# Loading and stepping the first block's odd spectra during the last chunk of a Fourier filter kernel

## The chip, the cores and the metric

The kernel runs on one core of a Trainium2 chip, in float32, as one launch. The metric is the device time of the whole kernel in microseconds (us): the median of three runs.

## What is computed

The input is an image batch of 4 x 56 x 56 positions with 128 channels. Layer 0 is a neighbourhood attention block (7 x 7 windows, four heads) with a dense block behind it. Layer 1 reads the same values as 3136 tokens for each of 4 images. It adds a small attention term and then a spectral filter, and it is the last part of the filter that matters here:

```python
Vf = jnp.fft.rfft(phi, n=n, axis=0)
Uf_p = jnp.fft.rfft(u, n=n, axis=1)
Uf_m = jnp.fft.rfft(u * sgn3, n=n, axis=1)
U_plus = jnp.fft.irfft(Vf[None, :, :, None] * Uf_p[:, :, None, :], n=n, axis=1)[:, :sl]
U_minus = jnp.fft.irfft(Vf[None, :, :, None] * Uf_m[:, :, None, :], n=n, axis=1)[:, :sl]
...
out = jnp.einsum('btkd,k,kde->bte', U_plus, s, Mpp)
out = out + jnp.einsum('btkd,k,kde->bte', U_minus, s, Mpm)
```

So the tokens are transformed to frequencies, at each frequency multiplied by 16 filters and mixed over the channels by matrices, and transformed back. Four such filters with different lengths are weighed and added to the tokens.

## The kernel before, in words

All engines have their own queues and wait for each other by semaphores: PE (matmuls), DVE, ACT and POOL (elementwise work), SP (DMA issue only). ACT issues DMAs too, in line with its other work. Every DMA that SP or ACT issues takes the next of eight semaphores in turn, and its issue waits until the DMA that had this semaphore before has landed. Hence at most eight are on their way.

**Chunks.** The 245 frequencies are worked off in 31 chunks of eight (`NCH = 31`, `FC = 8`). For chunk c, `fetch_tokens` (L1045) loads the transformed tokens into a tile `xc` (four loads of 256 KB on ACT, two tiles in turn), `tokens` (L1062, POOL) takes them apart into `v`, `make` (L1094) builds the frequency's matrices `g`: PE multiplies the filters `ph` with the mixing matrices `mc` into PSUM banks `pg`, and DVE and ACT copy them out. `product` (L1127) multiplies `v` and `g` into banks `py`. DVE forms sums and differences `ys`, and they are stored to the spectra `yd` in device memory (L1158): index 0 of `yd` for even spectra, 1 for odd ones. The loop at L1225 interleaves, in eight steps u, `make` of chunk c + 1 with `product` of chunk c. `g` lies in two large places in turn.

**The way back.** The rest is the inverse transform, for two blocks ("pair" 0 and 1) of two filters ("j") each. It needs all frequencies, in two halves of 128 ("fh" 0 and 1, from frequency 0 and from 117, so only half 1 needs the last chunk). For each block the odd spectra come first, then the even ones (L1350). `fetch_back` (L1172) brings one block, parity and half: eight loads of 512 KB on SP into a ring tile, which takes the place of a `g`: ring 0 (half 0) that of chunk 29, ring 1 (half 1) that of chunk 30. `odd` and `even` (L1273, L1257) do butterfly steps on DVE, in place: four operations of 128 x 1024 for each j of an odd half, and eight of 128 x 2048 down to 128 x 512 for each j of an even one. `products` (L1283) multiplies them on PE with tables of waves into eight PSUM banks: for the odd part 8 phases x 4 matmuls for each half, for the even part 8 x 2. Half 0 goes through all phases first, half 1 then closes the banks, and DVE adds each closed bank to the tokens in a tile `xo` (L1305). That sum frees the bank for the next part. The tables come through ACT: the odd table of half 0 takes the place of the mixing matrices `mc` (L1186), that of half 1 the tile `io`, the two even ones the tiles `ie`. `xo` is loaded by SP and stored by ACT (L1309).

**What sets the order.** Up to the first steps of the chunks the order is that of the code. After `order.close()` (L1223) a scheduler places the instructions on each queue by its own reckoning, except those marked with `keep_in_program_order` (the token loads, L1054). In the last chunk (c = 30) the loop's else-branch asks for the odd table of half 0 and for ring 0: odd, then even (L1232 to L1235):

```python
waves_back[0] = odd_waves(0, 0)
ring_tile()
for par in (1, 0):
    ready[par] = fetch_back(0, par, 0)
```

Of the kernel before, what the change touches and what calls it, by code (L numbers as in the profile page):

```python
# [9 lines left out]
FP = mybir.dt.float32  # L10
AF = mybir.ActivationFunctionType
ALU = mybir.AluOpType
AX = mybir.AxisListType
PSUM = bass.MemoryType.PSUM
DRAM = bass.MemoryType.DRAM

B, H, W, C = 4, 56, 56, 128
# [27 lines left out]
L = N // PH  # L45
R = NF // PH
RT = (0, R - C)
# [3 lines left out]
NCH = -(-R // FC)  # L51
SKIP = NCH * FC - R
FB = 4
CW = FC * PH * 2
# [6 lines left out]
def conv_attn_hybrid_kernel(ctx: ExitStack, tc: tile.TileContext, a: dict, out: bass.AP):  # L61
    nc = tc.nc
# [7 lines left out]
    yd = dram.tile([2, R, C + 8, C], FP, name="yd")  # L70
# [972 lines left out]
    filters_in, fetched, made, spectra, sums = {}, {}, {}, {}, {}  # L1043

    def fetch_tokens(c, j=None):  # L1045

        n = NP * B
        if c not in fetched:
            fetched[c] = cp.tile([C, n, CW], FP, tag="xc", name=f"xc{c}")
        x = fetched[c]  # L1050
        src = ud.rearrange("j b c w -> c (j b) w")[:, :, CW * c : CW * (c + 1)]
        if j is not None:
            part = slice(B * j, B * (j + 1))
            load = nc.scalar.dma_start(x[:, part], src[:, part])  # L1054
            if c > 1:
                tc.keep_in_program_order(load)
            return

        for part in (slice(n - B), slice(n - B, n)):
            nc.sync.dma_start(x[:, part], src[:, part])  # L1060
# [103 lines left out]
    ring, ready, waves_back = [], {}, {}  # L1164
# [4 lines left out]
        pool = gpools[(NCH + len(ring)) % 2]  # L1169
        ring.append(pool.tile([C, 2, 4, 2, PAIR], FP, tag="g", name=name))  # L1170

    def fetch_back(pair, par, fh):  # L1172
        y = ring[fh][:, 1 - par]

        for m in range(4):
            for r in range(2):
                row = 16 * (2 * m + r) + 8 * pair
                nc.sync.dma_start(
                    y[:, m, r],
                    yd[par, RT[fh] : RT[fh] + C, row : row + 8].rearrange("f n e -> f (n e)"),  # L1180
                )
        return y.rearrange("f m s (j x) -> f j m s x", j=2)

    def odd_waves(pair, fh, pool=None):
        if pool is None:
            t = mc.rearrange("c e d -> c (e d)")[:, : 32 * L]  # L1186
        else:
            t = pool.tile([C, 32 * L], FP, tag="io", name=f"io_{pair}_{fh}")
        nc.scalar.dma_start(t, a["itab_odd"][pair, fh])
        return t.rearrange("f (j k m r p n) -> f j k m r p n", j=2, k=2, m=2, r=2, p=2)  # L1190

    chunks = ExitStack()
    with tc.tile_pool(name="last", bufs=1, side="right") as own, tc.tile_pool(
        name="weigh", bufs=1, side="right"
# [9 lines left out]
        run(extra)  # L1204


    cp = chunks.enter_context(tc.tile_pool(name="w3", bufs=2, side="right"))
    filters_of(0)
    fetch_tokens(0)
# [4 lines left out]
    front.close()  # L1214

    gpools = [ctx.enter_context(tc.tile_pool(name=f"wg{i}", bufs=1)) for i in range(2)]
    ps_g = chunks.enter_context(tc.tile_pool(name="ps_g", bufs=6, space=PSUM))
    ps_y = chunks.enter_context(tc.tile_pool(name="ps_y", bufs=2, space=PSUM))
    for u in range(8):
        make(0, u)  # L1220
        if u % 2:
# [2 lines left out]
    PIECES = (1, 2, 5, 6)  # L1224
    for c in range(NCH):  # L1225
        if c + 1 < NCH:
            if (c + 1) % FB == 0:
                filters_of((c + 1) // FB)
            tokens(c + 1)
        else:  # L1230

            waves_back[0] = odd_waves(0, 0)  # L1232
            ring_tile()
            for par in (1, 0):
                ready[par] = fetch_back(0, par, 0)  # L1235
        for u in range(8):
            if c + 1 < NCH:
                make(c + 1, u)

                if c + 2 < NCH and u in PIECES:  # L1240
                    fetch_tokens(c + 2, PIECES.index(u))
            product(c, u)
    chunks.close()


    tokens_out = out.rearrange("b n p c -> b (n p) c")
    with tc.tile_pool(name="w4", bufs=1) as wp, tc.tile_pool(
        name="ps_t", bufs=8, space=PSUM
    ) as ps_t:
        ring_tile()  # L1250

        def butterfly(u, v):

            nc.vector.tensor_tensor(u, u, v, ALU.add)
            nc.vector.scalar_tensor_tensor(v, v, -2.0, u, ALU.mult, ALU.add)

        def even(y):  # L1257

            butterfly(
                y[:, :2].rearrange("f m s x -> f (m s) x"),  # L1260
                y[:, 2:].rearrange("f m s x -> f (m s) x"),
            )
            butterfly(y[:, 0], y[:, 1])
            butterfly(y[:, 2, 0], y[:, 3, 1])
            butterfly(y[:, 2, 1], y[:, 3, 0])
            return (
                [y[:, 0, 0], y[:, 0, 1]],
                [y[:, 3, 1], y[:, 2, 1]],
                [y[:, 1, 0], y[:, 1, 1]],
                [y[:, 2, 0], y[:, 3, 0]],  # L1270
            )

        def odd(y):  # L1273


            butterfly(y[:, :2, 0], y[:, 2:, 1])
            butterfly(y[:, :2, 1], y[:, 2:, 0])
            return (
                [y[:, 2, 1], y[:, 0, 1], y[:, 3, 1], y[:, 1, 1]],
                [y[:, 0, 0], y[:, 2, 0], y[:, 1, 0], y[:, 3, 0]],  # L1280
            )

        def products(pair, phases, terms, xos, dst):  # L1283


            banks = {}
            for fh in range(2):
                for j, p, *what in phases:
                    if fh == 0:
                        banks[j, p] = ps_t.tile([L, B, C], FP, tag="t", name=f"pi_{pair}_{j}_{p}")  # L1290
                    of = terms(fh, j, *what)
                    for k, (it, z) in enumerate(of):
                        nc.tensor.matmul(  # L1293
                            banks[j, p],
                            it,
                            z,
                            start=(fh == 0 and k == 0),
                            stop=(fh == 1 and k == len(of) - 1),
                        )
                    yield  # L1300
                    if fh == 0:
                        continue
                    xo = xos[j][:, :, p, :]
                    o = 2 * pair + j
                    nc.vector.scalar_tensor_tensor(  # L1305
                        xo, banks[j, p], on[:L, o : o + 1], xo, ALU.mult, ALU.add
                    )
                    if dst and p == 6:
                        nc.scalar.dma_start(dst[j], xos[j].rearrange("n b p e -> n b (p e)"))  # L1309
# [6 lines left out]
        for pair in range(2):  # L1316
# [7 lines left out]
            ys, xos = {}, []  # L1324
            ios = [
                waves_back[0] if pair == 0 else odd_waves(pair, 0),
                odd_waves(pair, 1, wp),
            ]
# [3 lines left out]

            def even_loads():
                for fh in range(2):
                    t = wp.tile([C, 16 * L], FP, tag=f"ie{fh}", name=f"ie_{pair}_{fh}")
                    nc.scalar.dma_start(t, a["itab_even"][pair, fh])
                    ies.append(t.rearrange("f (j p r n) -> f j p r n", j=2, p=4, r=2))
                ys[0, 0] = fetch_back(pair, 0, 0) if pair else ready[0]
                ys[0, 1] = fetch_back(pair, 0, 1)
                for j in range(2):  # L1340
                    xo = wp.tile([L, B, PH, C], FP, tag=f"xo{j}", name=f"xo_{pair}_{j}")
                    for b in range(B):
                        nc.sync.dma_start(
                            xo[:, b].rearrange("n p e -> n (p e)"), here[j][:, b]
                        )
                    xos.append(xo)
# [3 lines left out]
            for par, step, phases in ((1, odd, odd_phases), (0, even, even_phases)):  # L1350
                zs = {}
                for fh in range(2):
                    for j in range(2):
                        zs[fh, j] = step(ys[par, fh][:, j])
                        for _ in range(4):
                            next(behind, None)
                for _ in behind:
                    pass
                if par and pair:
                    even_loads()  # L1360

                def terms(fh, j, *what, zs=zs, ios=ios, ies=ies):
                    if len(what) > 1:
                        kind, i = what
                        return [
                            (ios[fh][:, j, kind, m, r, i], zs[fh, j][kind][2 * m + r])
                            for m in range(2)
                            for r in range(2)
                        ]
                    return [(ies[fh][:, j, what[0], r], zs[fh, j][what[0]][r]) for r in range(2)]  # L1370

                behind = products(pair, phases, terms, xos, None if par else into)
# [108 lines left out]
```

## Time and profile before

| | us |
|---|---|
| three runs: median (lowest to highest) | 1965.07 (1964.43 to 1971.44) |
| the profiled execution: its own time / its span | 1977.2 / 1975.4 |
| mean granted TensorE clock over the span | 0.976 of full speed |
| busy: PE / weight loads / DVE / ACT / POOL | 1885.4 / 1225.9 / 1202.1 / 1023.8 / 908.6 |
| steady chunks, for each 25 us from 1700 to 1775: PE / DVE busy | 24.8 to 25.0 / 17.9 to 18.4 |
| way back, 1775 to 1975: mean rate of the loads while they run | 240 to 409 GB/s |

Durations, waits and DMA shares come from one profiled execution; the median comes from runs without the profiler. A group in a view reads: start, duration, engine, line, operation, tiles written and read, shape, count, and in brackets the idle time ahead of it with what ended it. PE work on float32 stands in the profile as two records for each matmul of the code. PEld is PE's weight load, DVEq and the like the engine's queue.

### The profile page before, as it was taken

The page shows a single profiled execution, that of the slowest core. Times are in us where ns is not written, and L with a number is a line of the kernel's source. Part 1 is how long each engine was busy: PE and PEld are TensorE (multiplying, and loading weights), DVE is VectorE, ACT ScalarE, POOL GpSimd, SP SyncE. Part 2 cuts the span into 40 slices and gives each one's busy share as a digit, 9 for nine tenths or more (in the row PEclk, how much of TensorE's full clock was granted, in tenths as well). Part 3 has the DMA queues.
Part 4 walks back from the last instruction along what each step waited for, and adds up shares of the span by engine and source line. Part 5 has one row for each costly group of instructions (what it writes and reads, how often), then busy time and mean ns, then how long its engine had stood idle before and what let it go on. Part 6 is the DMA issues. An engine that isn't in the chain of part 4 may idle for free.

```text
span 1975.4 us, 57869 instructions
## 1 busy us (share of the span) xinstructions
PE 1885.4 (95%) x24220; PEld 1225.9 (62%) x24220; DVE 1202.1 (61%) x2749; ACT 1023.8 (52%) x2311; POOL 908.6 (46%) x1441
## 2 busy tenths in 40 slices
PE   7998999999999999999999999899999999996998
PEld 4555555565555565555565445788888888883333
DVE  3765644455645456544565664677777777765983
ACT  2666675556685656675555433455555555550000
POOL 2443321365321565222473026788888887770000
PEclk9898999899999999999999999999999999998999
DMA  3122000054000153000254628344444444449981
GB/s 104 33 89 68 2 1 1 19 182 158 2 1 1 31 198 129 1 1 1 83 172 158 203 80 294 99 126 132 126 130 127 126 131 125 128 140 392 355 308 66
DMA packets 184848, 223.48 MB, mean 113 GB/s; under 512 B 13016, under 2 KB 161561, under 8 KB 181996
## 3 DMA queue, kind: packets, MB, share of 16 engines
q1 hardware_dynamic: 107792, 129.07, 20.9%
q10 hardware_dynamic: 74444, 57.70, 9.4%
q0 software_dynamic: 2352, 33.01, 4.2%
q8 instruction: 191, 3.13, 0.6%
q14 instruction: 69, 0.57, 0.1%
HBM read 141.77 MB, written 77.97 MB: 111 GB/s over the span
## 4 chain that ended last, share of the span: by engine, by line
PE 78%; issue 7%; DVE 6%; DMA 5%; ACT 3%; POOL 1%; SPq 0%; ACTq 0%; DVEq 0%; POOLq 0%
PE pg L1103 14%; PE py L1139 13%; PE pi L1293 6%; PE px L716 5%; PE ppt L825 4%; PE pl L769 4%; PE ph L557 3%; PE pf L548 3%; PE par L650 3%; PE pav L882 3%; PE pv L845 3%; DMA ring<-yd 1%; DMA ud<-ab 1%; PE pav L430 1%; PE pk L489 1%
## 5 line engine op out<-in xcount | busy, mean ns | idle before, releaser
L809 POOL TENSOR_SCALAR p<-p,den 112x280 f32<-112x280 f32 x448 | 214.8, 497 | 481.0 <-PE ppt L825 226.6
L1121 DVE COPY g<-pg 128x512 f32<-128x512 f32 (+1 forms) x496 | 319.7, 690 | 147.3 <-PE pg L1103 147.2
L1119 ACT COPY g<-pg 128x512 f32<-128x512 f32 (+1 forms) x496 | 263.9, 584 | 232.9 <-PE pg L1103 232.9
L1103 PE MATMUL pg<-ph,mc 32*128 32x128 f32 x7936 | 296.2, 284 | 5.7 <-DVE g L1121 5.7
L796 ACT ACTIVATE p<-p,low 112x280 f32<-112x280 f32 x448 | 231.1, 517 | 94.0 <-DVE low L782 93.6
L1103 PEld LDWEIGHTS pg<-ph,mc 32*128 32x128 f32 x7936 | 248.4, 187 | 46.1 <-issue 37.3
L1139 PE MATMUL py<-g,v 128*32 128x128 f32 x7840 | 274.6, 281 | 1.3 <-issue 1.0
L1139 PEld LDWEIGHTS py<-g,v 128*32 128x32 f32 x7840 | 219.2, 152 | 30.5 <-issue 1.8
L782 DVE CUSTOM_DVE_ANT_0 p<-pl,bias 112x280 f32<-112x280 f32 x448 | 174.8, 445 | 15.1 <-PE pl L769 3.1
L832 DVE COPY pt<-ppt 120x448 f32<-120x448 f32 x112 | 69.3, 619 | 111.3 <-PE ppt L825 110.5
L825 PEld LDWEIGHTS ppt<-ident,p 112*120 112x120 f32 x896 | 99.6, 138 | 59.9 <-issue 39.6
L825 PE MATMUL ppt<-ident,p 112*120 112x112 f32 x896 | 127.5, 263 | 8.5 <-POOL p L809 4.1
L724 POOL TENSOR_TENSOR ab<-ab,w 128x496 f32<-128x496 f32 x60 | 74.6, 1243 | 105.4 <-ACT w L723 60.6
L716 PE MATMUL px<-tab,tok 98*128 98x496 f32 x256 | 117.8, 606 | 5.4 <-ACT tok L710 3.2
L832 ACT COPY pt<-ppt 120x448 f32<-120x448 f32 x224 | 87.1, 444 | 48.8 <-PE ppt L825 48.7
L769 PE MATMUL pl<-kt,qt 32*112 32x280 f32 x896 | 96.0, 444 | 11.9 <-ACT qt L508 5.7
L557 PE MATMUL ph<-ln_m,w_fc 128*128 128x448 f32 x224 | 102.5, 548 | 1.6 <-DVE ln_m L538 1.5
L548 PE MATMUL pf<-h,w_fc 128*128 128x448 f32 x224 | 100.8, 540 | 0.0
L565 ACT ACTIVATE h<-ph,b_fc 128x448 f32<-128x448 f32 x112 | 69.3, 633 | 60.5 <-PE ph L557 58.7
L882 PE MATMUL pav<-pt,v 120*32 120x112 f32 x1792 | 87.4, 267 | 0.0
L570 DVE SCALAR_TENSOR_TENSOR x<-pf,b_fc,x 128x448 f32<-128x448 f32 x28 | 19.1, 684 | 112.0 <-PE pf L548 112.0
L716 PEld LDWEIGHTS px<-tab,tok 98*128 98x128 f32 x256 | 48.6, 198 | 56.6 <-issue 42.2
(241 smaller groups left out, 3403.3 us busy)
## 6 DMA issues: line engine op xcount, KB each, us to landing
ring<-yd SPq DMA_DIRECT2D x64, 512.0 KB
ud<-ab POOLq DMA_DIRECT2D x16, 1984.0 KB, 8.8
xc<-ud ACTq DMA_DIRECT2D x120, 256.0 KB
tab<-in_tab SPq DMA_DIRECT2D x160, 189.9 KB
yd<-ys SPq DMA_DIRECT2D x118, 256.0 KB
mat<-in_M_phi_plus SPq DMA_DIRECT2D x16, 512.0 KB
mat<-in_M_phi_minus SPq DMA_DIRECT2D x16, 512.0 KB
x<-in_x SPq DMA_DIRECT2D x28, 224.0 KB
```

The source lines that it names most:

```text
L548: nc.tensor.matmul(po[:, :GT], late["w_fc2"][:, i, :], hts[g - 1][i], start=(i == 0), stop=(i == 3),)
L557: nc.tensor.matmul(ph[:, :GT], w_fc1[:, i * C : (i + 1) * C], lnm[:, g * GT : (g + 1) * GT], start=True, stop=True,)
L716: nc.tensor.matmul(ps, toks[i // 4][:, i % 4, :], next(tab), start=True, stop=True)
L769: nc.tensor.matmul(pls[h][:TQ, :KEYS], qts[b, g][hs, t * TQ : (t + 1) * TQ], kt[hs, r0 : r0 + KR, c0 : c0 + KC], start=True, stop=True,)
L782: nc.vector.tensor_tensor_reduce(out=f["p"][:, h, :], in0=f["pls"][h][:TQ, :KEYS], in1=bias[:, h, :], scale=-1.0, scalar=3.0e38, op0=ALU.a ...
L796: nc.scalar.activation(f["p"][:, h, :], f["p"][:, h, :], AF.Exp, bias=f["low"][:, h : h + 1], scale=-1.0, accum_out=f["den"][:, h : h + 1],)
L809: nc.gpsimd.tensor_scalar(f["p"][:, h, :], f["p"][:, h, :], f["den"][:, h : h + 1], 1.0, ALU.mult, ALU.mult)
L825: nc.tensor.transpose(ppt[:, i, :], of, ident[:TQ, :TQ])
L1103: nc.tensor.matmul(banks[rg][:, q, :], mc[r, 4 * u + q, :], t[r, at : at + CW], start=True, stop=True,)
L1119: nc.scalar.copy(into, src)
L1121: nc.vector.tensor_copy(into, src)
L1139: nc.tensor.matmul(py[32 * m : 32 * m + 32, f - f0, :], weights(v, 1 - r, f, slot), g[:, (2 * slot + r) * FC + f, :], start=(r == 0), stop ...
```

## The change

The odd spectra of block 0, half 0, j = 0 (eight pieces of 256 KB) are no longer part of ring 0. They go to two tiles `early0` and `early1` of the pool that holds the tokens `xc`, which now outlives the chunks. The four pieces of `early0` are loaded by ACT during chunk 29's products, at the four steps where the token loads of a further chunk would stand; the four of `early1` by SP at the start of the last chunk. Their steps are two butterflies, one ahead of the last chunk's loop and one after its step u = 5, both kept in program order on DVE, as are the steps of j = 1. Ring 0 keeps the pieces of j = 1. The even spectra of half 0 are asked for behind the odd ones of half 1 in the code. The odd table of half 0 is loaded in two pieces, the even tables take the places of the token tiles (so of `early0` and `early1`), and the inverse matmuls use the banks of the chunks' two PSUM pools instead of a pool of their own.

In the issue order of the changed program, everything up to the last chunks stands as before. On SP, `early1`'s four loads stand ahead of the stores of chunk 29's first sums; then come the eight smaller loads of ring 0, four even loads of ring 0, eight odd loads of ring 1, the other four even ones of ring 0, and the rest as before. On DVE the steps of `early0` stand ahead of the last chunk's first sums and those of `early1` ahead of its last sums.

```diff
-            fetched[c] = cp.tile([C, n, CW], FP, tag="xc", name=f"xc{c}")
+            fetched[c] = xp.tile([C, n, CW], FP, tag="xc", name=f"xc{c}")
...
+    def spectrum_of(par, fh, m, r, at, n):
+        row = 16 * (2 * m + r) + at
+        of = yd[par, RT[fh] : RT[fh] + C, row : row + n]
+        return of.rearrange("f n e -> f (n e)")
...
-    def fetch_back(pair, par, fh):
+    def fetch_back(pair, par, fh, first=0):
         y = ring[fh][:, 1 - par]
         for m in range(4):
             for r in range(2):
-                row = 16 * (2 * m + r) + 8 * pair
                 nc.sync.dma_start(
-                    y[:, m, r],
-                    yd[par, RT[fh] : RT[fh] + C, row : row + 8].rearrange("f n e -> f (n e)"),
+                    y[:, m, r, first * C :],
+                    spectrum_of(par, fh, m, r, 2 * B * pair + first, 2 * B - first),
                 )
...
+    halves = {}
+    def fetch_early(half, queue, i):
+        if half not in halves:
+            halves[half] = xp.tile([C, 4, B * C], FP, tag="xc", name=f"early{half}")
+        r = half if i < 2 else 1 - half
+        load = queue.dma_start(halves[half][:, i], spectrum_of(1, 0, i, r, 0, B))
+        if half == 0:
+            tc.keep_in_program_order(load)
...
+        n = 32 * L // parts
+        for part in range(parts):
+            here = slice(n * part, n * (part + 1))
+            nc.scalar.dma_start(t[:, here], a["itab_odd"][pair, fh][:, here])
...
+    def butterfly(u, v, hold=lambda i: i):
+        hold(nc.vector.tensor_tensor(u, u, v, ALU.add))
+        hold(nc.vector.scalar_tensor_tensor(v, v, -2.0, u, ALU.mult, ALU.add))
...
+    xp = ctx.enter_context(tc.tile_pool(name="xc", bufs=2, side="right"))
...
-            waves_back[0] = odd_waves(0, 0)
+            for i in range(4):
+                fetch_early(1, nc.sync, i)
+            waves_back[0] = odd_waves(0, 0, parts=2)
             ring_tile()
-            for par in (1, 0):
-                ready[par] = fetch_back(0, par, 0)
+            ready[1] = fetch_back(0, 1, 0, first=B)
+            butterfly(halves[0][:, :2], halves[0][:, 2:], tc.keep_in_program_order)
...
+                elif c + 2 == NCH and u in PIECES:
+                    fetch_early(0, nc.scalar, PIECES.index(u))
             product(c, u)
+            if c + 1 == NCH and u == 5:
+                butterfly(halves[1][:, :2], halves[1][:, 2:], tc.keep_in_program_order)
+    z0, z1 = ([h[:, i] for i in range(4)] for h in (halves[0], halves[1]))
+    first = [z0[2], z1[0], z0[3], z1[1]], [z0[0], z1[2], z0[1], z1[3]]
...
-                        banks[j, p] = ps_t.tile([L, B, C], FP, tag="t", name=f"pi_{pair}_{j}_{p}")
+                        pool, tag = (ps_g, "g") if len(banks) < 6 else (ps_y, "y")
+                        banks[j, p] = pool.tile([L, B, C], FP, tag=tag, name=f"pi_{pair}_{j}_{p}")
...
-                    t = wp.tile([C, 16 * L], FP, tag=f"ie{fh}", name=f"ie_{pair}_{fh}")
+                    t = xp.tile([C, 16 * L], FP, tag="xc", name=f"ie_{pair}_{fh}")
...
-                ys[0, 0] = fetch_back(pair, 0, 0) if pair else ready[0]
+                ys[0, 0] = fetch_back(pair, 0, 0)
...
-                        zs[fh, j] = step(ys[par, fh][:, j])
+                        if (pair, par, fh, j) == (0, 1, 0, 0):
+                            zs[fh, j] = first
+                            continue
+                        behind_sums = (pair, par, fh) == (0, 1, 0)
+                        hold = {"hold": tc.keep_in_program_order} if behind_sums else {}
+                        zs[fh, j] = step(ys[par, fh][:, j], **hold)
```

## The prediction

> **What bounds the kernel now.** I read first the table of busy time by stretch, to see which engine fills the tail, then the timeline of the tail, then the chain of work that ended last. Up to 1773 us the two programs issue the same work, but for eight small loads, so only the last 200 us matter.
>
> ```profile
> 1750.00:1775.00 25.00, 24.78 (x734) 21.53 (x732) 17.86 (x28) 13.56 (x25) 17.94 (x23) 1.00 0.45 139
> 1775.00:1800.00 25.00, 9.39 (x223) 7.12 (x216) 11.35 (x12) 1.18 (x2) 0.00 (x0) 0.74 1.01 360
> 1850.00:1875.00 25.00, 25.00 (x60) 9.64 (x59) 21.31 (x25) 0.00 (x0) 0.00 (x0) 1.00 1.02 404
> 1925.00:1950.00 25.00, 25.00 (x59) 9.57 (x58) 13.79 (x18) 0.00 (x0) 0.00 (x0) 1.00 0.00 1
> ```
>
> Columns: stretch, its length, busy time of PE, weight loads, DVE, ACT, POOL, then granted clock, DMA share, GB/s. PE is full but for one hole at 1775 to 1800. The DMA engines are full from there to about 1910, and less than half busy before. So the tail has two bounds side by side: PE, and the stream of loads.
>
> ```profile
> 1773.60 1.28 DVE L1155 TENSOR_TENSOR ys<-ya,py 128x512 f32<-128x512 f32 x2
> 1778.55 1.29 DVE L1155 TENSOR_TENSOR ys<-ya,py 128x512 f32<-128x512 f32 x2 [3.66 <-issue]
> 1780.72 2.00 PE L1139 MATMUL py<-g,v 128*32 128x128 f32 x63 [0.44 <-issue]
> 1782.82 1.28 DVE L1155 TENSOR_TENSOR ys<-ya,py 128x512 f32<-128x512 f32 x2 [2.99 <-PE py L1139]
> 1791.02 2.36 DVE L1254 TENSOR_TENSOR ring<-ring 128x1024 f32<-128x1024 f32 x2 [6.91 <-DMA yd<-ys]
> 1797.29 29.30 PE L1293 MATMUL pi<-ring,mc 128*98 128x512 f32 x64 [14.57 <-DMA ring<-yd]
> 1828.07 4.10 PE L1293 MATMUL pi<-ring,io 128*98 128x512 f32 x9 [1.48 <-DVE ring L1255]
> 1883.97 27.71 PE L1293 MATMUL pi<-ring,mc 128*98 128x512 f32 x64 [0.73 <-DVE xo L1305]
> ```
>
> The last product ends at 1782.72; the first inverse matmul starts at 1797.29, 14.57 us later. Two more waits follow: 1.48 us for the odd steps of frequency half 1, and 0.73 us before block 1. (The profile shows two records a matmul: 64 records are 32 matmuls.)
>
> ```profile
> 1784.14 9.04 DMA yd<-ys
> 1812.71 9.25 DMA ring<-yd
> 1866.84 10.53 DMA ring<-yd
> 1883.97 82.66 PE pi L1293 x192
> ```
>
> In the chain, the final stores of spectra take 9.04 us (to 1793.18), the last odd load of half 1 lands at 1821.96, and block 1's odd load of half 1 at 1877.37. From 1883.97 PE runs 192 records without a gap. A hole that is closed at 1783 is therefore worth its length only if the loads for 1828 and 1884 also come sooner.
>
> **The change, part by part** (in the profiled execution's own time, span 1975.4, its run 1977.2 us).
>
> *Early loads and steps.* Eight loads of 256 KB move ahead of the last products: four on ACT in the place of token fetches, four on SP. While DMA was 45% busy, such loads are cheap. The ACT queue gets four of them, and two halves of a table in place of one whole: five more issues of 0.36 us, from about 1759 on. Eight DMA semaphores go round, and each issue waits for the landing before it on its own; so three of ACT's wait for SP's early loads. Behind them wait the copies of g, and behind these PE's last products. ACT idles 0.5 to 1.1 us before each pair of copies (its timeline), so I take 0 and a bound of +1 us (below nothing: excluded, an added issue frees nothing). The four steps on DVE are 128x1024; a pair of that size takes 2.36 us (row at 1791.02). The holes they go to are 3.66 and 2.99 us, so they cost nothing if their loads are in by about 1776. If the last piece, issued near 1771 behind half a table, takes the whole table's path (issued 1769.33, 7.59 us to land by the trace), it lands near 1778.5 and pushes the sums behind it by 1 to 2 us. POOL gets no new work; SP's early loads wait for POOL's last reading of the token tile (1765.4) and hold back two stores that nobody waits for yet.
>
> *First inverse matmuls.* They find their spectra and half a table in place, and banks free since the copies of g: start at 1783.0, 14.3 us sooner. The clock: the granted clock fell to 0.5 in the hole, and the first 64 records took 29.30 us against 27.71 at 1883.97. So half 0 ends at 1783.0 + 27.7 = 1810.7.
>
> *Half 1, odd.* Ahead of its eight loads stand eight requests of 256 KB less in size and four of 512 KB fewer: 8 x 0.26 + 4 x 0.52 = 4.2 MB, at the 410 GB/s of the stretch 1808 to 1822 10.2 us: last landing 1821.96 - 10.2 = 1811.8. (The issue order shows that only half of the even requests really go behind the odd ones; four stay ahead.) The other bound: these loads must wait for the final stores (1793.2 before). From there 4.2 MB, beside a table of 1.6 MB and two of 0.8, is 7.4 MB at 401 GB/s (stretch 1783 to 1808): 18.4 us, 1811.6. Both agree. The steps ahead of the first matmul took 4.7 us (1823.39 to 1828.07); part of them now starts before the last landing, so PE goes on at about 1816. It was ready at 1810.7: a new wait of 5.3 us. Against 1828.07 the lead is now 12.
>
> *Even steps.* PE ends the odd part at 1816 + 27.6 = 1843.6. It then needs PSUM banks whose sums stand on DVE between the even steps of half 1, which stand behind those of half 0. The last four even loads of half 0 come behind the odd ones: 2.1 MB, 5.1 us alone and 9.6 us beside block 1's table (3.7 MB at the 385 GB/s of 1826 to 1836); I take 8, since the table is asked for a little later: 1819.8. The steps of half 0 are two times 9.4 us (two operations of 2.25, two of 1.15, four of 0.65, from the rows of 2048, 1024 and 512): 1838.5. Up to the third sum there are two of 2.25, three sums of 0.7, two of 1.15 and three of 0.65: 10.9, thus 1849.4. PE asks for that bank at 1843.6 + 2 x 1.73 = 1847.1: 2.3 us of wait. The fourth and fifth sums come 3.6 and 3.0 us later, PE asks every 1.73: 3.2 more. Sum 5.5, bounds 0 and 9. The even part ends at 1843.6 + 27.7 + 5.5 = 1876.8, where it was 1883.24.
>
> *Block 1.* Its first matmul waits for even sums that stand on DVE behind the first odd steps of both halves, hence for a load of half 1: landed 1877.37, PE 1883.97, 6.6 us later. That load has 2.1 MB less ahead of it, 5.2 to 5.4 us at 404 to 390 GB/s; the fuller queue around 1776 to 1782 (share 0.89 to 0.97) gives up to 2 more, a stream run dry while SP waits for the stores takes up to 2. I take 6.4: 1871.0 + 6.6 = 1877.6, just behind PE. From there 82.66 us and the end as before; the sums of block 1's even part have over 6 us to spare. **Sum: 1883.97 - 1877.6, 6.4 us sooner**, a span of about 1969. The three runs' median is 1965.07, 12 under the profiled run; nothing in the sum scales with that, so 1965.07 - 6.5 = 1958.5.
>
> **Two rules against it.** *Small loads:* a load of 512 KB lands every 1.28 us with eight in flight (410 GB/s). The Trainium skill, DMA: Bandwidth & Descriptors, section Bandwidth, advises batches of at least 1 MiB, with 78% of peak at that size and little at small ones. By it, 2.1 MB in pieces half as large and a halved table would lose some tenths of their 5 us, about 1 us estimated; by the row nothing, as queued requests overlap. I keep 0 and put 1 into the range. *Clock:* in the trace the clock fell 4.2 us after the last product and rose 3.3 us after the restart. The skill, TensorE: Matmul & The Clock Gate, section What's actually happening, says that one idle window of some 3.4 us halves it. By the row's 4.2 us, and by the rule more so, my new 5.3 us wait can trip it again, for 29.30 - 27.71 = 1.6 us. As DVE and the loads, not PE, set the next steps, I count 0, and 1.6 as the bound.
>
> **Rivals.**
> - *The hole is simply gone* (18%). If the loads of half 1 land near 1806 and the even steps follow as closely, the lead stays 10 to 15 us: 1950 to 1955, about 1953. For: the time before 1775 has free DMA. Against: 1.02 of DMA share from 1783 on, and DVE full between 1811 and 1861.
> - *The stream takes it back* (17%). Only 2.1 MB leave a full stream, and a dry spell of 3 to 4 us while SP waits for the stores cancels most of their 5.4: 1 to 3 us, about 1963. For: all loads queue behind one waiting SP instruction.
> - *Slower than before* (6%). The same place, worse: before, 16 requests could run ahead of the final stores; now 12 smaller ones (4.2 MB, 10.5 us) can. If the stores land after about 1800 instead of 1793, the stream stands still over 7 us, and everything behind it on SP moves back: about 1970 when they land at 1805. The deciding point is a dry spell longer than 7 us. The held order on DVE would feed this: sums that wait for an early piece delay those stores.
> - That it doesn't do what it says is true in part: half of the even requests stay ahead; this is in the sum.
>
> **How the numbers follow.** Main case 59%: 5 to 9 us, 1956 to 1960, with 1958.5 the likeliest. With rivals and bounds (ACT +1, clock +1.6, even wait 0 to 9) the range is 1951.5 to 1964.5, which leaves out some 15%. About 0.5%, 9.8 us, is what a measurement can tell from no change: faster by more than that means below 1955.2, the first rival's larger part and a little of the main case, 22%; slower by more 3%; within it 75%.
>
> **What would show it.** Right: inverse matmuls start within 1 us of the last product; a new PE wait of 3 to 7 us at the first io table's matmuls; PE waits for DVE sums at the start of the even part; block 1 starts 5 to 9 us sooner, still 6 to 7 us behind a landing. Wrong: PE without any wait from the last product on (the first rival), DMA share below 0.8 somewhere in 1784 to 1800 (the second and third), products of the last chunk that take over 10 us instead of 9 (held steps), or a time before 1770 that differs.

## The result, and the profile after

Compared on one chip, 12 runs of each: the changed kernel 1969.21 us median (1957.58 to 1974.86), the kernel before 1969.75 (1964.35 to 1978.59), ratio 0.9968 with a 95% interval of 0.9944 to 0.9992. By the ratio that is 6.3 us faster (1.6 to 11.0), below the 0.5% that one can tell from no change; the two medians differ by only 0.5 us and the two means by 3.2. The prediction was 6.5 us (1965.07 to 1958.5), which lies in the interval. The absolute median lies above the predicted range. The kernel before, too, ran 4.7 us slower here than in its first three runs; shifted by that, the median stands at the range's upper end, and by the ratio (0.9968 of 1965.07 is 1958.8) in its middle.

The profiled execution of the changed kernel has a span of 1960.6 us (its own time 1962.35) against 1975.4. Only part of these 14.8 us belongs to the change: the last chunk's first product starts at 1764.34 and started at 1773.70, so 9.4 us lie ahead of it, where the two programs are alike but for a few early loads (in the runs below, alike up to there, it starts anywhere from 1758.6 to 1773.2). All comparisons below therefore count from that first product, written +t. The tail (from there to the end of the span) was 201.7 us and is 196.3: 5.4 us shorter. That agrees with the timed runs, but it is one execution of each kernel: the start of the inverse matmuls, here at +10.40, came at +10.2 to +13.1 in the eight profiled runs that share this order on DVE, so other executions of the changed kernel may have a tail up to 2.7 us longer (an estimate from this spread).

Timeline of the changed kernel, columns as in the prediction:

```profile
1764.34 5.49 PE L1139 MATMUL py<-g,v 128*32 128x128 f32 x192 [0.21 <-DVE g L1121]
1768.72 1.23 DVE L1213 TENSOR_TENSOR early<-early 128x1024 f32<-128x1024 f32 x1 [3.19 <-DMA ring<-yd]
1772.55 2.26 PE L1139 MATMUL py<-g,v 128*32 128x128 f32 x64 [2.73 <-DVE ys L1155]
1774.74 13.97 PE L1320 MATMUL pi<-early,mc 128*98 128x512 f32 x32
1788.55 13.90 PE L1320 MATMUL pi<-ring,mc 128*98 128x512 f32 x32
1808.89 29.30 PE L1320 MATMUL pi<-ring,io 128*98 128x512 f32 x64 [6.44 <-DVE ring L1214]
1813.17 4.49 DVE L1213 TENSOR_TENSOR ring<-ring 128x2048 f32<-128x2048 f32 x2 [0.93 <-DMA ring<-yd]
1838.02 3.60 PE L1320 MATMUL pi<-ring,ie 128*98 128x512 f32 x8
1841.94 1.96 PE L1320 MATMUL pi<-ring,ie 128*98 128x512 f32 x4 [0.32 <-DVE xo L1332]
1845.40 1.96 PE L1320 MATMUL pi<-ring,ie 128*98 128x512 f32 x4 [1.50 <-DVE xo L1332]
1848.26 20.84 PE L1320 MATMUL pi<-ring,ie 128*98 128x512 f32 x48 [0.90 <-DVE xo L1332]
1869.20 27.71 PE L1320 MATMUL pi<-ring,mc 128*98 128x512 f32 x64
```

The 14.57 us hole is gone: inverse matmuls follow the last product at once (+10.40 for +23.59, 13.2 us sooner). A new wait of 2.73 us stands ahead of the last products, one of 6.44 ahead of the io table, and three of 0.32, 1.50 and 0.90 in the even part. Block 1 starts at +104.86 for +110.27, 5.4 us sooner; from there nothing differs (91.4 us to the end in both).

The same in the table of busy time by stretch:

```profile
1775.00:1800.00 25.00, 25.00 (x59) 9.60 (x58) 5.93 (x6) 0.00 (x0) 0.00 (x0) 1.00 0.98 372
1800.00:1825.00 25.00, 18.56 (x40) 6.90 (x39) 21.00 (x16) 0.00 (x0) 0.00 (x0) 0.86 1.02 388
1825.00:1850.00 25.00, 22.28 (x51) 8.02 (x50) 25.00 (x27) 0.00 (x0) 0.00 (x0) 1.00 1.01 321
1850.00:1875.00 25.00, 24.90 (x59) 9.48 (x58) 25.00 (x27) 0.00 (x0) 0.00 (x0) 1.00 1.02 409
```

PE is full where it had 9.39 us of work, and has a hole of 6.4 us in the next stretch, with a granted clock of 0.86 there. DVE has 25.00 of 25 us in all three stretches from 1825 on; before it had 24.29, 21.31 and 23.65 there. The chain of work that ended last agrees:

```profile
1777.34 5.38 DMA yd<-ys
...
1783.17 10.69 DMA ring<-yd
1793.88 10.35 DMA ring<-yd
...
1808.89 22.44 PE pi L1320 x48
1831.35 2.28 DVE ring L1213
...
1868.48 0.67 DVE xo L1332
1869.20 82.66 PE pi L1320 x192
```

It runs through the last store of spectra, two odd loads of half 1, one behind the other on the same semaphore, PE's odd part, and then 38 us of DVE's steps and sums. In the kernel before, its link ahead of block 1 was a load (10.53 us).

### The profile page after: what moved, and what is told of

Same layout as the page of the kernel before. It is cut to its first block, busy times and chain, and to the rows that moved or that the text cites. A ratio compares the mean times of both kernels' runs of the same rounds, so it can differ in the third digit from the quotient of the medians.

```text
span 1960.6 us, 57886 instructions
## 1 busy us (share of the span) xinstructions
PE 1878.3 (96%) x24220; PEld 1222.1 (62%) x24220; DVE 1200.7 (61%) x2749; ACT 1023.6 (52%) x2311; POOL 908.2 (46%) x1441
## 4 chain that ended last, share of the span: by engine, by line
PE 78%; DVE 7%; issue 7%; DMA 3%; ACT 3%; POOL 1%; ACTq 0%; SPq 0%; DVEq 0%; POOLq 0%
PE pg L1103 14%; PE py L1139 13%; PE pi L1320 5%; PE px L716 5%; PE ppt L825 5%; PE pl L769 4%; PE par L650 3%; PE ph L557 3%; PE pf L548 3%; PE pav L882 3%; PE pv L845 3%; PE pav L430 1%; PE pk L489 1%; DVE p L782 1%; DMA ring<-yd 1%
## 5 line engine op out<-in xcount | busy, mean ns | idle before, releaser
L1103 PEld LDWEIGHTS pg<-ph,mc 32*128 32x128 f32 x7936 | 248.1, 187 | 46.1 <-issue 37.2
L796 ACT ACTIVATION_READ_ACCUMULATOR p<-p,low 112x1 f32 x448 | 83.7, 187 | 0.0
```

What stands on the lines that cost most here:

```text
L796: nc.scalar.activation(f["p"][:, h, :], f["p"][:, h, :], AF.Exp, bias=f["low"][:, h : h + 1], scale=-1.0, accum_out=f["den"][:, h : h + 1],)
L1103: nc.tensor.matmul(banks[rg][:, q, :], mc[r, 4 * u + q, :], t[r, at : at + CW], start=True, stop=True,)
```

## The experiments

Each of these was profiled once; e10, e11 and e12 were also timed. Single times of one kernel range over 0.7 to 0.9%, more than most of the effects, so the tail of the profile is read. Times in us from the first product of the last chunk; "even steps" is DVE's first 128x2048 step of half 0.

| | first inverse matmul | last store landed | last odd piece of half 1 | first io matmul (wait) | even steps | block 1 | end |
|---|---|---|---|---|---|---|---|
| before | 23.59 | 19.49 | 47.9 | 54.37 (1.48) | 38.00 | 110.27 | 201.7 |
| changed | 10.40 | 18.39 | 39.9 | 44.55 (6.44) | 48.83 | 104.86 | 196.3 |
| e1 | 8.09 | 21.57 | 43.2 | 47.74 (11.94) | 51.00 | 107.03 | 198.6 |
| e2 | 10.22 | 18.97 | 37.9 | 42.57 (4.63) | 48.44 | 105.42 | 196.7 |
| e3 | 13.14 | 20.76 | 44.0 | 48.64 (7.29) | left out | 107.12 | 198.4 |
| e4 | 12.61 | 20.84 | 43.3 | 48.00 (7.13) | 51.26 | 107.29 | 198.7 |
| e5 | 10.57 | 14.67 | 34.1 | 40.10 (1.82) | 50.72 | 106.75 | 199.7 |
| e6 | 9.33 | 14.56 | 34.7 | 42.04 (5.00) | 52.55 | 108.58 | 202.0 |
| e7 | 8.16 | 14.53 | 31.4 | 35.73 (0) | 46.63 | 101.57 | 192.9 |
| e8 | 12.87 | 20.89 | 43.0 | 54.91 (0) | 50.94 | 110.48 | 201.8 |
| e9 | 11.25 | 18.25 | 48.0 | 49.31 (10.35) | 30.70 | 105.71 | 197.1 |
| e10 | 8.79 | 14.03 | 30.7 | 36.33 (0) | 42.35 | 97.17 | 190.4 |
| e11 | 8.62 | 15.91 | 32.7 | 37.03 (0.70) | 44.20 | 119.75 | 211.3 |
| e12 | 11.33 | 16.70 | 33.3 | 39.82 (0) | 44.87 | 99.69 | 195.8 |

My theory at the start of these: PE, DVE's row of steps and block 1's loads all reach block 1 at about the same time, so that relieving one brings nothing. The rivals: the loads alone, DVE alone, or the held order.

**e1: the steps of early0 behind the first sums.**

```diff
-            butterfly(halves[0][:, :2], halves[0][:, 2:], tc.keep_in_program_order)
...
+            if c + 1 == NCH and u == 3:
+                butterfly(halves[0][:, :2], halves[0][:, 2:], tc.keep_in_program_order)
```

> The changed kernel, but the steps of early0 stand on DVE behind the first sums of the last chunk instead of ahead of them. Times are counted from the first product of the last chunk (there: first inverse matmul +10.40, first io matmul +44.55 after 6.44 of wait, block 1 +104.86). Theory (three chains meet at block 1: PE itself, DVE's row of steps and sums, the loads of block 1): the 2.73 us wait of the products is gone, first inverse matmul at about +9.0; the last stores land up to 1.4 us sooner, the first io matmul at +43 to +44.5, block 1 no more than 1.4 sooner. Rival (the held order costs what was given back): block 1 at least 3 us sooner. If the steps, now closer to the last sums, hold those up, the stores land no sooner and the gain stays with the first 1.4 us of PE, which then waits longer.

The products lost their wait, and the first inverse matmul came at +8.09. But the io table's wait grew to 11.94: the scheduler put a fifth even request ahead of half 1's odd ones, and the last store landed at +21.57, 9.6 us after its issue. Block 1 came 2.2 us later, which none of the theories said. Two things changed, so this run doesn't price the held order; e12 does, in e10's order of loads.

**e2: the even tables behind the spectra.** Their two loads move from ACT to SP, behind the even spectra.

> The changed kernel, but block 0's two even tables (0.8 MB each) are asked for on SP behind all its spectra, not on ACT beside the odd spectra of half 1. Theory: between the landing of the stores (+18.4) and the last odd piece of half 1 (+39.9) 7.4 MB move; without 1.6 MB of these it lands 4 to 4.6 us sooner, PE's wait at the io table falls from 6.44 to about 2, the clock does not fall, so the odd part of half 1 takes 27.7 and not 29.1, and the even part starts 5 to 6 us sooner. Block 1 is then held by its own loads (last piece at +98.8, PE 6 us later) and comes no more than 1.5 us sooner. Rival 1 (the waiting for the stores alone sets the landing): the wait stays at 6 us or more. Rival 2 (what PE loses in half 1 is what the change lost): block 1 comes 4 us or more sooner.

The last odd piece landed 2.0 us sooner, not 4, in part because the store landed 0.6 later; the wait fell to 4.63 only. Block 1 came 0.6 us later: DVE began its even steps at the same time (+48.4) and its sums stood one step later in the scheduler's order (PE waited 4.24 us for them). Both rivals are out. That the tables take part of that time is right: from store to last odd piece 18.9 us for 21.5.

**e3: without half 0's even steps on DVE. e4: without the reload of block 1's first table.**

```diff
...
-                        zs[fh, j] = step(ys[par, fh][:, j], **hold)
+                        if (pair, par, fh) == (0, 0, 0):
+                            zs[fh, j] = even(ys[par, fh][:, j], False)
+                        else:
+                            zs[fh, j] = step(ys[par, fh][:, j], **hold)
```

```diff
-            nc.scalar.dma_start(t[:, here], a["itab_odd"][pair, fh][:, here])
+            if pair == 0 or fh == 1:
+                nc.scalar.dma_start(t[:, here], a["itab_odd"][pair, fh][:, here])
```

> Leaves out the even steps of block 0, half 0 (16 operations of DVE, 18.8 us by the before kernel's rows), so the even part's output is not the reference's. Theory (loads, DVE and PE meet at block 1): PE's waits for sums in the even part (2.72 us) go, and PE's even part ends 2.7 us sooner, but block 1 starts at most 1.2 us sooner, since its last odd piece of half 1 still lands at about +98.8. Rival (DVE alone is the bound): block 1 starts 2.7 us sooner, at PE's own limit.

> Leaves out the reload of the odd table of block 1, half 0 (1.6 MB; its matmuls use block 0's table, so block 1's odd part is not the reference's). Theory: block 1's last odd piece lands up to 4 us sooner, but DVE's row of steps and sums is unchanged, so block 1 starts at most 1 us sooner and the waits of the even part stay near 2.7. Rival (the loads alone are the bound): block 1 starts 2 us or more sooner.

In both, the held step cost more than in the changed kernel (first inverse matmul at +13.14 and +12.61), so block 1 is read from there: 94.0 us later in e3 and 94.7 in e4, against 94.5. DVE with 18.8 us less to do gains 0.5 us: PE's own work, with its wait for half 1's odd pieces, is as long. In e4 block 1's last odd piece landed at +96.1 for +98.8, 83.5 for 88.4 us after the first inverse matmul, and nothing came of it. So the loads of block 1 do not set its start.

**e5: all even requests behind the odd ones. e6: that, with e1's steps.**

```diff
...
-                ys[0, 0] = fetch_back(pair, 0, 0)
+                hold = {} if pair else {"hold": tc.keep_in_program_order}
+                ys[0, 0] = fetch_back(pair, 0, 0, **hold)
```

> The changed kernel, with all eight even requests of half 0 held behind the odd ones of half 1 on SP (four stood ahead). Times count from the first product of the last chunk. Theory (half 1 waits for the landing of the last stores, which share the queues with the loads asked for ahead of them): the last store lands 2 to 3 us sooner (+15.5 to +16.5 for +18.4), the last odd piece of half 1 about as much sooner (+36 to +38 for +39.9), the first io matmul at +41 to +43 (+44.55). Block 1 at most 1.5 us sooner, since the same bytes are asked for before it. Rival 1 (dry spell): while SP waits for the stores nothing else is queued, the DMA share falls below 0.8 between +9 and +20, the whole stream moves back, and block 1 starts 1 to 4 us later. Rival 2 (what is lost at half 1 is what the change lost): block 1 starts over 2 us sooner.

> As e5, and the steps of early0 stand behind the first sums of the last chunk, as in e1. In e1 the products lost their wait, but the last store landed at +21.6, behind four even loads and with a semaphore that one of the small loads held. Theory: without even loads ahead of them the stores land at +14 to +17, half 1's last odd piece 19 to 22 us later, the first io matmul at +38 to +42. Rival (the stores' own issue, which waits for semaphores, sets their landing): they land at +19 or later, and the first io matmul comes at +44 or later. Block 1: at most 2 us sooner than in the changed kernel by the theory of three chains, over 3 if only half 1's wait counts.

The stores landed 3.7 us sooner (e5: +14.67) and half 1's odd pieces 5.8 us sooner, so stores and loads do share: PE's wait fell to 1.82. Yet block 1 came 1.9 us later in e5, as its rival 1 had it, and 3.7 in e6, which nothing had foretold. The timeline of e5 shows why:

```profile
1820.31 4.49 DVE L1213 TENSOR_TENSOR ring<-ring 128x2048 f32<-128x2048 f32 x2 [7.27 <-DMA ring<-yd]
1841.48 29.61 PE L1320 MATMUL pi<-ring,ie 128*98 128x512 f32 x64 [4.09 <-DVE xo L1332]
1876.34 29.24 PE L1320 MATMUL pi<-ring,mc 128*98 128x512 f32 x64 [5.25 <-DVE xo L1332]
```

DVE stood idle for 7.27 us until the even pieces of half 0 had landed, and PE then waited twice for its sums. From this step to block 1 are 56.03 us. The same 56.03 us lie between them in the changed kernel, e1, e4 and e6. So the theory gets a name for its middle chain: the landing of half 0's last even piece, and DVE's row behind it. The dry spell is real (in e5 the DMA share is 0.75 at 1780 to 1784 and 0.89 in the next 4 us), and it acts by that landing. Another part is the order: by the semaphores for which DVE waits, its first even step stands behind the 25th load into the ring tiles in e5 (landed at +50.6) and behind the 26th in e6 (+52.5), where the changed kernel has the 24th (+48.7). The two parts aren't told apart here. From e5 to e6 the steps of `early0` alone were moved, and block 1 came 1.8 us later: freeing the products did not pay by itself here.

**e7: as e6, with the even tables behind the spectra too. e10: as e7, with block 1's first odd table on SP, behind block 0's tokens.**

```diff
...
-            nc.scalar.dma_start(t[:, here], a["itab_odd"][pair, fh][:, here])
+            if pair and fh == 0:
+                tc.keep_in_program_order(
+                    nc.sync.dma_start(t[:, here], a["itab_odd"][pair, fh][:, here])
+                )
+            else:
+                nc.scalar.dma_start(t[:, here], a["itab_odd"][pair, fh][:, here])
```

> As e6, and the two even tables of block 0 are asked for on SP behind the even spectra. Theory: half 1's last odd piece lands another 3 to 4 us sooner than in e6 (1.6 MB fewer beside it), PE's wait at the io table is below 2 us and the clock stays up (odd part of half 1 in 27.7). Block 1 at most 2 us sooner than in the changed kernel, its start set by its own loads or by DVE. Rival: block 1 over 3 us sooner.

> As e7 (even spectra and even tables behind, early0's steps later), and block 1's odd table of half 0 (1.6 MB) is asked for on SP behind the token loads of block 0, not on ACT beside the even spectra. In e7 block 1 started at +101.6, 54.9 us after DVE's even steps of half 0 (+46.6, at a landing). Theory (that landing and DVE's row behind it set block 1): the landing comes 3 to 4 us sooner, block 1 at +97.5 to +99.5, some 6 us sooner than in the changed kernel. Rival (block 1's own loads set it): at +101 or later, as these have the same bytes ahead of them. Timed against the kernel before: the tail is then 11 to 13 us shorter than before's 201.7, so about 0.6% faster, if the early part of the program is the same.

In e7 the wait at the io table is gone, and the clock stays up there (27.71). Even steps start at +46.63, block 1 at +101.57, 3.3 us sooner than in the changed kernel: more than the theory's 2, as the rival expected; the loads of block 1 were not the limit that I held them for. In e10, with 1.6 MB fewer beside the even pieces, DVE starts at +42.35, and block 1 follows 54.82 us later:

```profile
1814.18 4.49 DVE L1218 TENSOR_TENSOR ring<-ring 128x2048 f32<-128x2048 f32 x2 [3.81 <-issue]
1839.76 29.41 PE L1326 MATMUL pi<-ring,ie 128*98 128x512 f32 x64 [3.97 <-DVE xo L1338]
1869.00 27.63 PE L1326 MATMUL pi<-ring,mc 128*98 128x512 f32 x64
```

Of the 54.82 us, DVE's steps up to the sum for which PE waits (3.97 us) take 25.6, and PE's even part behind it 29.2. Block 1 is at +97.17, 7.7 us sooner than in the changed kernel, though block 1's last odd piece of half 1 landed only at +101.0, after that start. Timed: ratio to the kernel before 0.9949 (0.9931 to 0.9966), the tail 11.3 us shorter than before.

**e8: PE repeats 16 matmuls in the place of the wait.**

> The changed kernel, but PE repeats the 16 matmuls of j = 1, half 0 (with the same result) ahead of the io table's matmuls, so that its 6.4 us of wait are filled with work. Theory: the granted clock stays at 1.00, the odd part of half 1 takes 27.7 us and not 29.1 to 29.3, and the even part starts 1.5 us sooner. Block 1 starts at most 1 us sooner, since DVE and the loads are no sooner. Rival: the 1.5 us of clock go through to block 1. If the odd part still takes over 29 us, the time is not the clock's.

```profile
1799.77 13.90 PE L1336 MATMUL pi<-ring,mc 128*98 128x512 f32 x32
1813.50 27.63 PE L1323 MATMUL pi<-ring,io 128*98 128x512 f32 x64
```

No wait, and the odd part took 27.63 us, not 29.3: the 1.6 us are the clock's. The filling was too long by some 7 us (PE started at +54.91; the last odd piece had landed at +43.0, and in the changed kernel PE starts 4.7 us behind it), so block 1 came later, and this run tells nothing of the rest.

**e9: the reordering undone.** All eight even requests are asked for in the last chunk, as before the change.

> The changed kernel with the reordering undone: all eight even requests of half 0 stand ahead of the odd ones of half 1 on SP. Times count from the first product of the last chunk. In the changed kernel and in four of the runs above, block 1 starts 56.03 us after DVE begins its even steps of half 0 (there +48.8, when the last even piece has landed), with DVE busy all the time. Theory (DVE's row from the landing of half 0's even pieces sets block 1, unless PE's own work or block 1's loads do): half 1's odd pieces land about 5 us later (+44 to +46) and the first io matmul comes at +48.5 to +51; DVE's even steps start sooner (+37 to +42), so DVE no longer sets block 1; PE does (io matmul + 55 to 57) or its loads: +104 to +107, within 2 us of the changed kernel. Rival 1 (the reordering brings the gain): +108 or later. Rival 2 (the reordering only costs): +102 or sooner.

```profile
1771.56 3.80 PE L1139 MATMUL py<-g,v 128*32 128x128 f32 x64 [2.02 <-DVE ys L1155]
1813.35 29.10 PE L1321 MATMUL pi<-ring,io 128*98 128x512 f32 x64 [10.35 <-DVE ring L1213]
1842.28 27.63 PE L1321 MATMUL pi<-ring,ie 128*98 128x512 f32 x64
1869.75 27.63 PE L1321 MATMUL pi<-ring,mc 128*98 128x512 f32 x64
```

DVE's even steps start at +30.70, and the io table's wait is 10.35 us; behind it PE waits no more. Block 1 is at +105.71, 0.85 us later than in the changed kernel, and that is what the products and their wait took more here: counted from the first inverse matmul it comes after 94.46 us in both. So in these executions the reordering as it was made brings nothing: it trades PE's wait for odd pieces against waits for DVE. The gain comes from the rest of the change, the early loads and steps.

**e11: POOL does half 0's even steps for j = 1.**

> As e10, and POOL, idle in the tail, does the even steps of block 0, half 0, j = 1 (9.4 us of DVE; 12 operations, estimated at 26 us from POOL's rows of 128x512 at 1.32 us and 128x1024 at 1.09). Theory: DVE's row to block 1 is 9 us shorter, PE's 8.8 us of waits in the even part shrink below 3, block 1 starts at +91 to +96, unless its loads hold it at +99 or more (rival 1). Rival 2: POOL and DVE slow each other when both work on these tiles; then DVE's rows of 2.25 and 2.35 us become longer and block 1 starts at +98 or later.

Ratio 1.004 (1.0012 to 1.0068), block 1 at +119.75. Rival 2 was right, and far stronger than I thought. DVE, and then POOL, in the timeline:

```profile
1813.30 6.47 DVE L1223 SCALAR_TENSOR_TENSOR ring<-ring 128x2048 f32<-128x2048 f32 x1
1811.20 6.42 POOL L1218 TENSOR_TENSOR ring<-ring 128x2048 f32<-128x2048 f32 x1 [46.72 <-DMA ie<-in_itab_even]
1817.71 7.29 POOL L1220 TENSOR_SCALAR ring<-ring 128x2048 f32<-128x2048 f32 x1
1856.02 30.66 PE L1331 MATMUL pi<-ring,ie 128*98 128x512 f32 x64 [24.51 <-DVE xo L1343]
```

The DVE step of 2.28 us takes 6.47 and ends 2.15 us behind POOL's first operation, as if it had waited for its end (1817.62); PE waits 24.51. The Trainium skill, SBUF — State Buffer, section Who interferes with whom, says that a DVE instruction with two SBUF inputs contends with a GpSimd (POOL) instruction that reads SBUF, for a shared pair of ports that only one of them holds at a time; the row agrees. All butterfly steps on DVE have two such inputs.

**e12: e10 with the held order back**, the one difference between the two.

> As e10, with one difference: early0's steps stand ahead of the first sums of the last chunk again, as in the changed kernel. The order on SP, ACT and PE is that of e10. Times count from the first product of the last chunk. e10: products end +8.85, last store +14.0, first inverse matmul +8.79, block 1 +97.2, end +190.4. Theory (the held order costs what it holds the products and the stores up, and all of it goes through when the landing of half 0's even pieces and DVE's row behind it set block 1): products wait 2.5 to 4.5 us, first inverse matmul at +10.3 to +13, the last store 0.5 to 4 us later, block 1 and the end later by about what the stores lose, 1 to 4 us. Rival 1 (the held order is free, as predicted): first inverse matmul at +9, block 1 within 0.5 us of e10. Rival 2 (the wait is real, but the stores land no later, so it is hidden): first inverse matmul later, block 1 within 0.5 us of e10.

```profile
1768.32 1.23 DVE L1218 TENSOR_TENSOR early<-early 128x1024 f32<-128x1024 f32 x1 [3.37 <-DMA ring<-yd]
1772.15 3.00 PE L1139 MATMUL py<-g,v 128*32 128x128 f32 x64 [2.91 <-DVE ys L1155]
1775.08 14.92 PE L1325 MATMUL pi<-early,mc 128*98 128x512 f32 x32
```

DVE waits 3.37 us for an early piece, PE behind it 2.91, and the clock falls (14.92 for 13.97). First inverse matmul 2.5 us later, last store 2.7, block 1 2.5: in this pair of executions the held order goes through in full. The end came 5.4 us later; the other 2.9 are a wait for a sum in block 1's even part that grew from 1.71 to 2.77 and tripped the clock there (44 records in 20.82 for 19.12). The timed ratio, 0.9932 (0.9905 to 0.9959), overlaps with that of e10 and doesn't tell the two apart.

## Why the prediction was right, and where not

**The size was right**, as far as 12 runs of each tell (1.6 to 11.0 us) and the profile does (5.4). The tail's ledger on PE, changed against before: the hole closed 14.6; less 1.4 for products held up; less 3.4 in half 0 and its wait (34.15 us from first inverse to first io matmul for 30.78); less 1.6 for the odd part of half 1 (29.13 for 27.55, clock); less 2.8 in the even part (31.18 for 28.35). It leaves 5.4; predicted were 6.4. The ledger counts PE's time and names no causes. That the sum came so near is in part luck: at the end of the odd part PE stood 3.8 us behind the prediction (+73.7 for 1843.6, +69.9), and the even part, 2.0 us shorter than expected (31.18 for 33.2), gave that much back. The even part of the kernel before, from which 27.55 and 28.35 are counted:

```profile
1855.62 27.63 PE L1293 MATMUL pi<-ring,ie 128*98 128x512 f32 x64
```

- **Early loads and steps, "I take 0": wrong.** It cost 1.4 us here. By the trace the last piece, issued on ACT at 1761.50, landed at 1768.43, +4.1. Its two steps take 2.4 us, so the first sums, which stood at +4.85 before, came at +6.79, and the products that need their bank waited. The prediction had both ends, free if the loads are in by 1776 (+2.3), sums pushed by 1 to 2 us if the last lands at 1778.5 (+4.8), and took the wrong one. In eight profiled runs with this order the first inverse matmul came at +10.2 to +13.1, in the five without it at +8.1 to +9.3. Between e10 and e12 it is worth 2.5 us through to block 1. In the changed kernel's own order of loads its price at block 1 isn't shown: e1 and e6, without it, gained nothing there. The prediction had named the sign: products that take over 10 us (10.47).
- **First inverse matmuls and half 0: right.** At once behind the last product, in 27.7 us.
- **Half 1, odd: right in kind, 1.1 short.** Predicted wait 5.3, measured 6.44; the last piece came at +39.9 (predicted 1811.8, +38.1).
- **Small loads: the row was right.** Pieces of 256 KB landed one every 0.67 us in the changed kernel (from +7.39 to +10.73), those of 512 KB one every 1.28: by the byte 4% slower, 0.2 us for the eight pieces of ring 0.
- **Clock, counted at 0 with a bound of 1.6.** It fell, and the wait of 6.44 us cost PE the 1.6 (e8). Whether any of it reached block 1 isn't shown: PE waited 2.72 us for DVE's sums behind it, and DVE was busy without a hole from 1825 on.
- **Even steps.** 5.5 us of waits predicted, 2.72 measured; DVE's even steps of half 0 came later than thought (landing at +48.7 for 1819.8, +46.1) but PE came later, too.
- **Block 1, "bound by the load of half 1": the step whose mechanism failed.** That load did come 6.4 us sooner, as taken: its last piece landed at +98.8 for +105.2. (The prediction read 1877.37 as its landing; by the semaphores that is the seventh of eight pieces, and the last landed at 1878.88. In the same way the last odd piece of block 0 landed at 1821.64, not 1821.96.) PE followed the last piece 5.1 us later before, and 6.0 us later in the changed kernel, so the number came out near, but by chance: with that load 4.9 us sooner (e4, from the first inverse matmul) nothing moved, and in e10 block 1 started ahead of it. Before, DVE had sat idle for 1.35 us until the seventh piece was there; now it had 25.00 us of work in every 25. What sets block 1 is the landing of half 0's even pieces and 55 to 56 us of work behind it (DVE's steps and sums, in e7, e10 and e12 with PE's even part at their end), and, as long, PE's own way from half 1's odd pieces (e3, e9). The odd pieces, and the even ones asked for behind them, come after the last stores of spectra. Moving the even requests changes the one for the other (e5, e9); fewer bytes beside both (e7, e10) shortened the two together.
- **Rivals.** "The hole is simply gone" fell to the full stream, as said against it. "The stream takes it back" is partly true, but not by a dry spell: the DMA share from 1784 to 1800 was 0.95 to 1.02 in the changed kernel, and in e10, with 0.48 at 1784 to 1788, block 1 still came soonest of all. "Slower than before" did not come near: the stores landed at +18.4, sooner than before.

What stays open: why the last piece of `early0` lands at anything from +3.4 to +5.8 in the eight runs (the wait ahead of the last products, 1.7 to 4.4 us, grows with it), how much of the even pieces' delay in e5 and e6 is the dry spell's, and whether the reordering would pay in a kernel without the held order.

## What to carry to other kernels

When a hole on the busiest engine is closed, write down the next landing on which each engine depends, and how much unbroken work follows it: here two such chains, PE's own (block 1 at +105.71 in e9) and DVE's (+104.86 in the changed kernel), were within a microsecond of each other, so a gain of 13 us at one place was worth 5 at the end. Of requests in a full stream, ask which are not needed yet: what helped was to take tables out of the way of both landings, not to swap them. A step that waits for data hands its wait on when it stands ahead of work that could be done and whose result others wait for: here DVE's wait of 3.2 us for a piece became a wait of 2.73 us on PE.

## What the runs showed of the hardware

- DVE and POOL working on SBUF at the same time: a DVE step of 128x2048 with two inputs 6.47 us for 2.28 (e11). A POOL operation with one input took 7.29 beside DVE; what it takes alone isn't measured.
- The granted clock in these 14 traces falls to 0.50 and comes back on a grid of 3.41 us: in the tails, as long as PE had work, it stayed low for 3.41, 6.83, 10.24, 13.65 or 27.31 us. What decides is PE's idle time within one such stretch, not the length of a wait (worked out by cutting every tail at these steps). At full clock, each stretch with 2.02 us or more idle was followed by half clock, each with 1.87 or less was not; between them, stretches with 1.92 (e2) and 1.97 (e12) were, one with 1.97 (e5) was not. So the wait of 2.02 us in e9, all in one stretch, tripped the clock (64 products in 3.80 us for 2.00), and the 2.73 us of the changed kernel, cut into 1.33 and 1.40, did not (64 products in 2.26 us, granted clock 1.00). Every wait of 3.5 us or more cost 1.4 to 3 us. The Trainium skill, TensorE: Matmul & The Clock Gate, section What's actually happening, gives one idle window of about 3.4 us; in these runs some 2 us of idle time in a stretch of that length were enough.
- The stores of spectra share the DMA engines with queued loads: 256 KB took 5.4 to 8.5 us to land among them in the changed kernel, 2.6 to 6.2 with fewer loads queued (e10).
